# Re-timing three pieces of work at the seam between projections and attention

## The chip, the cores and the metric

The kernel runs on one core of a Trainium2 chip. The metric is the time of one execution on the device, in microseconds (us); less is better. The core has five engines that run side by side, each working through its own list of instructions in order: TensorE (PE, matrix products), VectorE (DVE), ScalarE (ACT), GpSimd (POOL) and SyncE (SP), which here issues every transfer. An engine that meets an instruction whose inputs are not ready stands still, and everything behind that instruction waits with it. The same is true of the list of transfers on SP.

## The reference

The input `x` has 1024 rows of 512 columns. It is normalized by rows, and the result goes into an attention and into a feed-forward network whose weights are stored as small integers with scales. The output is `x` plus the attention, multiplied by a gate made of the network:

```python
def reference(x, Wq, Wk, Wv, Wo, q_norm_w, k_norm_w, gate_w, ..., down_s):
    xn = layernorm(x)
    # attention: 32 query heads, 8 key/value heads of 128 columns
    q, k, v = heads(xn @ Wq.T), heads(xn @ Wk.T), heads(xn @ Wv.T)
    q, k = rmsnorm(q, q_norm_w), rmsnorm(k, k_norm_w)
    scores = q @ k.T / sqrt(128)            # four query heads share one key head
    bias = where(col > row, -1e30, slope[head] * (col - row))
    s = (softmax(scores + bias) @ v) @ Wo.T
    # feed-forward
    gate, up, down = (dequantize(w, scale, zero) for ...)
    g = silu((silu(xn @ gate) * (xn @ up)) @ down)
    return x + s * g
```

## The kernel before

**Precision.** Each product is made of three float16 products: an operand is split into a high half and a low half (the rest), and high x high, high x low and low x high are added up. `mm3` issues these three, at lines 114, 115 and 116, so all large products after the feed-forward part carry these line numbers; the tile names (`ps_q`, `s`, `av`, `op`) tell them apart.

**Stages.** The feed-forward part runs first, to about 215 us. Then come twelve projections, in groups of three: keys and values of two heads (`kv`), and queries of the one and of the other key group (`q`). They are numbered 0 to 11: kv0, q0, q1, kv1, q2, q3, and so on; number 9 is kv3, number 10 is q6, and number 11, the last, is q7. Each has eight row tiles, so there are 96 tiles (`TILES`). Attention follows in 256 steps, one for each pair of a unit (key group, block of 256 queries, head) and a tile of 128 queries. A key group has 32 steps. The first eight steps of the softmax run ahead: they are interleaved with the 16 tiles of the last two projections (`early_tile`, one step per two tiles), so the loop over `step` starts at step 8.

**What a projection leaves to be finished.** After the four tiles of one half, `queue_half` puts the finishing of that half on a calendar (`finishing`, a list per value of `clock[0]`, which advances by one with every tile or step). The finishing consists of `inverse` (VectorE, over the sums of squares `ss` that ScalarE made), for projections 0 to 9 `root` (ScalarE's square root), `newton` (POOL), then for each tile `normalize` (POOL, L650), `halves` (VectorE, L662 and L663, for keys L661 too), one clock later `transposed` (a transposing DMA on SP, L671) and two clocks after that `store` (a DMA to DRAM, L676 for queries, L678 for keys). The tile `f`, which ScalarE's copy at L592 fills and `halves` reads last, comes from four rotating buffers.

For the last projection the calendar is set by hand: `LAST_ROOTS` and `LAST_PAIRS` give the entry at which a half's root or a tile's halves are made, counted from `TILES`. Step 8 runs at clock `TILES`, so an entry n falls into step n + 8. The pairs of the last projection stay in SBUF, and `last_queries` transposes them directly when `LAST_QUERIES` says.

**A step of attention.** `scores` (TensorE, tile `s`), `biased` (VectorE, L896), `exponentials` (ScalarE, L902), `split_hi` (ScalarE, L921, the high half of p), `split_lo` (VectorE, L930, the low half), the latter ending with the transposition of p on SP (L938, or L933 for the first query block, tile `pT`). Nine steps after its scores, `values` multiplies transposed p with the values (tile `av`); `heads_hi` and `heads_lo` split the outcome (L964, L969), and `out_proj` multiplies it with the output weights, which are loaded by `load_wo` (L852), scaled on POOL (L855) and split on ScalarE (L861) and POOL (L862). In each key group from the second to the last but one the order of query blocks is 2, 3, 0, 1, with eight steps each.

**The main loop.** It prepares projection k + 1 (`prepare`: norms at tile 1, the split of its weights from tile 2 to 6), loads the weights of projection k + 2 in four quarters at tiles 0 to 3 (L500) and squares them on ScalarE from tile 5 on (L508). At the start of projection 9 it loads keys (L817), values (L821) and the first queries (L825) of attention. The weights of projections and half of the tiles `pT` share the two buffers of the tag "wide".

Of the kernel before, what the change touches and what calls it, by code (L numbers as in the profile page):

```python
# [10 lines left out]
F32 = mybir.dt.float32  # L11
# [10 lines left out]
P = 128  # L22
# [9 lines left out]
HT = NT // 2  # L32
# [21 lines left out]


LAST_ROOTS = {1: 24, 0: 36}
LAST_PAIRS = {4: 46, 5: 78, 6: 110, 7: 142, 2: 174, 3: 221, 0: 224, 1: 229}
LAST_QUERIES = {4: 217, 5: 219, 6: 225, 7: 227, 2: 233, 3: 235, 0: 241, 1: 243}

WO_SPLIT = 6  # L60
# [16 lines left out]
def attention_gated_by_ffn_kernel(ctx, tc, x, gu_w, gu_z, gu_s, dn_w, dn_z, dn_s, wq, wkv, wo, qnw, knw, out):  # L77
# [397 lines left out]
    clock, finishing = [0], {}  # L475
# [7 lines left out]
    def defer(steps, f):  # L483
        finishing.setdefault(clock[0] + steps, []).append(f)
# [4 lines left out]
    class Projection:  # L489
# [92 lines left out]
        def tile(self, t):  # L582
            n, half, r = self.n, t // HT, t % HT
            if r == 0:
                self.f[half] = fq.tile([P, HT, n, HD], F32, tag="f", name=f"f_{self.name}_{half}", bufs=4)
                self.ss[half] = fq.tile([P, HT, n], F32, tag="ss", name=f"ss_{self.name}_{half}", bufs=3)
                self.jk = wp.tile([P, NH, HD], BF16, tag="jk", name=f"jk_{self.name}_{half}")
            ps = ps1("o" if t % 2 else "m", f"ps_{self.name}_{t}")
            rows = slice(t * P, (t + 1) * P)
            for j in range(KT):  # L590
                mm3(ps, (xth[:, j, rows], xtl[:, j, rows]), (self.wh[:, j, :], self.wl[:, j, :]), j == 0, j == KT - 1)
            se.copy(self.f[half][:, r], ps[:, : n * HD].rearrange("p (g d) -> p g d", g=n))  # L592
            for i in range(n):
                se.activation(
                    self.jk[:, i],
                    ps[:, i * HD : (i + 1) * HD],
                    AF.Square,
                    scale=STEEPER[i] / Q_SCALE if self.kind == "q" else 1.0,
                    accum_out=self.ss[half][:, r, i : i + 1],
                )  # L600
            if self.kind == "kv":
                if t == 0:
                    self.v16 = vp16.tile([P, 2, NT, 2, HD], F16, tag="v16", name=f"v16_{self.i}")
                v16 = self.v16[:, :, t]
                vp = ps[:, 256:512].rearrange("p (g d) -> p g d", g=2)
                se.copy(v16[:, :, 0, :], vp)
                defer(1, lambda: ve.tensor_tensor(v16[:, :, 1, :], vp, v16[:, :, 0, :], ALU.subtract))
                if t == NT - 1:
                    defer(3, self.store_values)
# [5 lines left out]
        def inverse(self, half):  # L615

            m = HT * self.n
            a = fq.tile([P, m], F32, tag="ms", name=f"ms_{self.name}_{half}")
            y = fq.tile([P, m], F32, tag="inv", name=f"inv_{self.name}_{half}")
            w = fq.tile([P, m], F32, tag="nwt", name=f"nwt_{self.name}_{half}")  # L620
            ve.scalar_tensor_tensor(
                a.rearrange("p (t g) -> p t g", t=HT),
                self.ss[half],
                1.0 / HD,
                self.eps.unsqueeze(1).to_broadcast([P, HT, self.n]),
                ALU.mult,
                ALU.add,
            )
            self.inv[half] = (y, a, w)
            if not self.by_root:  # L630
                rsqrt_seed(a, y)
# [48 lines left out]
    projections = []  # L680
# [102 lines left out]
    def queue_half(p, half):  # L783

        last = p is projections[-1]

        def due(steps, i, f):
            if last and i is None:
                c = TILES + LAST_ROOTS[half]
            elif last:  # L790
                c = TILES + LAST_PAIRS[half * HT + i] - 4
            else:
                c = clock[0] + (i or 0)
            finishing.setdefault(c + steps, []).append(f)

        due(0, None, lambda: p.inverse(half))
        if p.by_root:
            due(1, None, lambda: p.root(half))
            due(2, None, lambda: p.newton(half, True))
        else:  # L800
            for i in range(3):
                due((i + 1) // 2, None, lambda i=i: p.newton(half, i == 0))
        later = int(p.by_root)
        for i in range(HT):
            t = half * HT + i
            due(4 + later, i, lambda t=t: p.halves(t))
            due(2 + later, i, lambda t=t: p.normalize(t))
# [7 lines left out]
    def load_keys(g):  # L815
        kT[g] = ap1.tile([P, NT, 2, P], F16, tag="kT", name=f"kT{g}")
        sp.dma_start(kT[g].rearrange("p t a k -> p t (a k)"), kd[g // 2][:, g % 2])  # L817

    def load_values(g):
        vT[g] = ap1.tile([P, NT, 2, HD], F16, tag="vT", name=f"vT{g}")  # L820
        sp.dma_start(vT[g].rearrange("p t a d -> p t (a d)"), vd[g])  # L821

    def load_queries(g, qb):
        qT[g, qb] = ap1.tile([P, NQT, 2, NH, P], F16, tag="qT", name=f"qT{g}_{qb}", bufs=2)
        sp.dma_start(  # L825
            qT[g, qb].rearrange("p t a g q -> p t (a g q)"), qd[g][qb * NQT : (qb + 1) * NQT].rearrange("t p c -> p t c")
        )
# [77 lines left out]
    def split_hi(u, qt):  # L905
# [14 lines left out]
            p16[u] = both  # L920
        se.activation(p16[u, qt][:, :, 0, :], pf[u, qt], AF.Copy, scale=scale[:, qt : qt + 1])  # L921

    def split_lo(u, qt):
        p, h16 = pf.pop((u, qt)), p16.pop((u, qt))
        nk = p.shape[1]
        if qt == 0:
            pool, tag = (wide, "wide") if u % 4 < 2 else (pt_pool, "pT")
            pT[u] = pool.tile([P, NT, 2, QB], F16, tag=tag, name=f"pT{u}", bufs=2)
        hi, lo, scale = h16[:, :, 0, :], h16[:, :, 1, :], rows16[u][3][:, qt : qt + 1]
        ve.scalar_tensor_tensor(lo, p, scale, hi, ALU.mult, ALU.subtract)  # L930
        if u in p16:
            if qt == NQT - 1:
                sp.dma_start_transpose(  # L933
                    pT[u][:, :NQT].rearrange("p t a (i q) -> p (t a i) q", i=NQT),
                    p16.pop(u).rearrange("p t a i k -> p (t a i k)"),
                )
            return
        sp.dma_start_transpose(  # L938
            pT[u][:, :nk, :, qt * P : qt * P + P].rearrange("p t a q -> p (t a) q"), h16.rearrange("p t a k -> p (t a k)")
        )  # L940

# [175 lines left out]
    last_ps = None  # L1117
    relative(0)
    for k, p in enumerate(projections):
        if k == len(projections) - 3:  # L1120
            load_keys(0)
            load_values(0)
            for qb in blocks[0][1]:
                load_queries(0, qb)
        for t in range(NT):
            prepare(k + 1, t)
            if k + 2 < len(projections):
# [4 lines left out]
                    projections[k + 2].squares(i)  # L1132
            if t == HT:
                p.undo()
            if (k, t) == (len(projections) - 3, HT + 1):
                wo_squares_sums()

# [59 lines left out]
```

## Time and profile before

| | |
|---|---|
| three runs | 1060.75, 1058.24, 1058.08 us; median 1058.24 |
| profiled execution | 1055.74 us, its span 1054.0 us |
| engines busy, share of the span | PE 95%, DVE 84%, ACT 76%, POOL 40% |
| matmuls of the projections q0 to q7 | 238 to 482 us |
| scores of step 0, 8, 32, 64 start at | 432.5, 481.1, 540.1, 608.2 us |
| SP busy issuing, of each 10 us from 470, 480, 490 us | 10.0, 9.1, 9.5 us |

In the rows of the profile, "waits" name the engine and line that waited, behind the arrow the one that released it, then the total in us, how often, and the longest. Rows of the timeline have the start, the duration, the engine and line, the operation with its output and inputs, and in square brackets the idle time of the engine just before, with what ended it. SPq is SP's queue of transfers: its durations are the time that issuing one took, not the time of the transfer. "Windows" give, for a stretch of time, its length and the busy time of PE, PEld (weight loads), DVE, ACT and POOL with the count of instructions, then the granted clock of TensorE, the busy share of the DMA engines and their GB/s.

### The profile page before, as it was taken

To read this page: it belongs to the slowest core of one execution; us is meant where nothing else is said; L and a number is where in the kernel's file an instruction comes from. 1 tells how busy PE (TensorE), PEld (TensorE's weight loads), DVE (VectorE), ACT (ScalarE), POOL (GpSimd) and SP (SyncE) were. 2 spreads that over 40 slices of the span, in tenths; PEclk is the share of its full clock that TensorE was granted. 3 is DMA by queue.
4 is the path that set the end of the run, shared out by engine and by line. 5 is a ranking of instruction groups with operands and counts; after the bars stand their busy time and mean duration, and the time that the engine had idled before them with its cause. 6 is when DMAs were issued, how large, how long until landed. Compare 5 with 4: busy or idle time off the path is not lost.

```text
span 1054.0 us, 18375 instructions
## 1 busy us (share of the span) xinstructions
PE 999.9 (95%) x5913; PEld 585.8 (56%) x5913; DVE 882.7 (84%) x1745; ACT 800.5 (76%) x2160; POOL 420.8 (40%) x407
## 2 busy tenths in 40 slices
PE   7899899999999999898899999999999999999996
PEld 5444367854444444344566567566666666665563
DVE  7888997626888877887789899898998998979986
ACT  5777645778878787787789688797997888968862
POOL 1688654115555647371324215113142151340732
PEclk8999999999999999999999999999999999999999
DMA  6032349536998989989999999899998998999995
GB/s 204 30 120 91 99 135 307 203 121 170 216 274 176 250 205 242 263 181 225 222 193 222 190 200 219 168 227 203 191 215 185 215 210 185 219 227 200 232 188 131
DMA packets 455039, 204.39 MB, mean 194 GB/s; under 512 B 401506, under 2 KB 411038, under 8 KB 454942
## 3 DMA queue, kind: packets, MB, share of 16 engines
q1 hardware_dynamic: 454942, 203.21, 86.8%
q8 instruction: 46, 0.75, 0.3%
q14 instruction: 51, 0.42, 0.1%
HBM read 77.32 MB, written 27.27 MB: 99 GB/s over the span
## 4 chain that ended last, share of the span: by engine, by line
PE 59%; DVE 13%; ACT 10%; DMA 9%; issue 6%; POOL 2%; SPq 0%; DVEq 0%; ACTq 0%; POOLq 0%
PE gu_ps L267 6%; DMA pT<-p 5%; PE s L114 4%; PE s L116 4%; PE s L115 4%; PE op L116 3%; PE op L115 3%; PE op L114 3%; PE ps_q L115 3%; PE ps_q L116 3%; PE ps_q L114 3%; PE av L114 3%; PE av L115 3%; PE av L116 3%; DVE pf L896 2%
## 5 line engine op out<-in xcount | busy, mean ns | idle before, releaser
L930 DVE SCALAR_TENSOR_TENSOR p<-pf,row,p 128x1024 f16<-128x1024 f32 (+7 forms) x256 | 224.9, 878 | 21.4 <-ACT p L921 18.4
L902 ACT ACTIVATE pf<-pf,row 128x1024 f32<-128x1024 f32 (+7 forms) x256 | 197.4, 771 | 41.4 <-DVE row L896 36.9
L896 DVE CUSTOM_DVE_ANT_0 pf<-s,trel,cs 128x1024 f32<-128x1024 f32 (+7 forms) x256 | 207.0, 809 | 20.8 <-PE s L116 20.4
L921 ACT ACTIVATE p<-pf,row 128x1024 f16<-128x1024 f32 (+7 forms) x256 | 196.6, 768 | 6.9 <-DMA pT<-p 2.1
L114 PE MATMUL av<-pT,vT 128*128 128x256 f16 (+1 forms) x640 | 168.4, 263 | 21.0 <-DMA pT<-p 21.0
L115 PE MATMUL av<-pT,vT 128*128 128x256 f16 (+1 forms) x640 | 168.4, 263 | 0.0
L116 PE MATMUL av<-pT,vT 128*128 128x256 f16 (+1 forms) x640 | 168.2, 263 | 0.0
L114 PE MATMUL s<-kT,qT 128*128 128x512 f16 (+3 forms) x384 | 125.6, 327 | 4.8 <-DVE row L896 4.8
L115 PE MATMUL s<-kT,qT 128*128 128x512 f16 (+3 forms) x384 | 125.6, 327 | 0.0
L116 PE MATMUL s<-kT,qT 128*128 128x512 f16 (+3 forms) x384 | 123.9, 327 | 0.0
L855 POOL TENSOR_SCALAR wor<-wor,rvs 128x512 f32<-128x512 f32 x32 | 51.9, 1623 | 169.4 <-DMA wor<-in_wo 148.9
L115 PE MATMUL ps_q<-wl_q,xth 128*128 128x512 f16 x256 | 97.0, 379 | 3.6 <-DVE wl_q L565 3.6
L114 PEld LDWEIGHTS <-vT 128*128 128x128 f16 x640 | 62.9, 98 | 62.6 <-issue 13.0
L116 PE MATMUL ps_q<-wh_q,xtl 128*128 128x512 f16 x256 | 97.0, 379 | 0.0
L114 PE MATMUL ps_q<-wh_q,xth 128*128 128x512 f16 x256 | 97.0, 379 | 0.0
L114 PE MATMUL op<-woh,oh 128*128 128x512 f16 x248 | 94.0, 379 | 0.0
L115 PE MATMUL op<-wol,oh 128*128 128x512 f16 x248 | 94.0, 379 | 0.0
L116 PE MATMUL op<-woh,ol 128*128 128x512 f16 x248 | 94.0, 379 | 0.0
L964 ACT ACTIVATE oh<-av 128x256 f16<-128x256 f32 x128 | 47.7, 373 | 54.8 <-PE av L116 53.9
L115 PEld LDWEIGHTS <-vT 128*128 128x128 f16 x640 | 62.9, 98 | 40.9 <-issue 2.4
L650 POOL TENSOR_TENSOR f_q<-f_q,inv_q 128x512 f32<-128x512 f32 x64 | 80.1, 1275 | 1.0
L862 POOL TENSOR_TENSOR wol<-wor,woh 128x512 f16<-128x512 f32 x32 | 50.3, 1572 | 60.9 <-ACT woh L861 59.1
(194 smaller groups left out, 2263.9 us busy)
## 6 DMA issues: line engine op xcount, KB each, us to landing
qd<-tr_q SPq DMA_DIRECT2D x56, 256.0 KB, 3.4
qT<-qd SPq DMA_DIRECT2D x28, 512.0 KB, 4.5
wq<-in_wq SPq DMA_DIRECT2D x32, 256.0 KB, 4.0
wo_sq<-in_wo SPq DMA_DIRECT2D x8, 1024.0 KB, 8.9
wor<-in_wo SPq DMA_DIRECT2D x32, 256.0 KB, 3.5
gui<-in_gu_w SPq DMA_DIRECT2D x13, 512.0 KB, 4.0
wkv<-in_wkv SPq DMA_DIRECT2D x16, 256.0 KB, 4.0
vd<-v SPq DMA_DIRECT2D x8, 512.0 KB, 4.6
```

The costliest lines, as they stand in the source:

```text
L114: te.matmul(ps, lhsT=lh, rhs=rh, start=first, stop=False)
L115: te.matmul(ps, lhsT=lh, rhs=rl, start=False, stop=False)
L116: te.matmul(ps, lhsT=ll, rhs=rh, start=False, stop=last)
L267: te.matmul(banks[j][:, k, :], lhsT=w[:, j, ws], rhs=x[:, j, k * 512 : k * 512 + 512], start=x is xth, stop=x is xtl)
L650: ge.tensor_tensor(f, f, ib, ALU.mult)
L855: ge.tensor_scalar(wor[g, i], wor[g, i], rvs[:, g : g + 1], None, ALU.mult)
L862: ge.tensor_tensor(wol[g, i], raw, woh[g, i], ALU.subtract)
L896: ve.tensor_tensor_reduce(p, ps, trel[g][:, S - w :], cs[:, hh : hh + 1], 3e38, ALU.add, ALU.min, least[:, c])
L902: se.activation(p, p, AF.Exp, bias=least[:, c], scale=-1.0, accum_out=total[:, c])
L921: se.activation(p16[u, qt][:, :, 0, :], pf[u, qt], AF.Copy, scale=scale[:, qt : qt + 1])
L930: ve.scalar_tensor_tensor(lo, p, scale, hi, ALU.mult, ALU.subtract)
L964: se.activation(oh, av_ps[u], AF.Copy, scale=1.0 / P_SCALE)
```

## The change

Four edits go together. The finishing of q6's second half (the last projection but one) gets a calendar of its own: roots at entry 32, pairs at entries 44, 60, 76 and 92; the pairs of q7's second half and its third tile move from 46, 78, 110, 142, 174 to 108, 124, 140, 156, 172. The finishing of projections 0 to 9 is spread: the inverse one clock later, the root at 2 instead of 1, the Newton step at 4 instead of 2, normalization and halves two clocks later; `ss`, `ms`, `inv` and `nwt` get four buffers. As long as the clock is below `TILES`, the transposition of p is deferred by one clock, which puts it into the tile after the next. Keys and first queries are loaded at tile 4 of projection 9 instead of ahead of its first tile, and values at tile 4 of projection 10.

```diff
-LAST_PAIRS = {4: 46, 5: 78, 6: 110, 7: 142, 2: 174, 3: 221, 0: 224, 1: 229}
+LAST_PAIRS = {4: 108, 5: 124, 6: 140, 7: 156, 2: 172, 3: 221, 0: 224, 1: 229}
+
+LATE_ROOTS = 32
+LATE_PAIRS = [44, 60, 76, 92]
...
-                self.ss[half] = fq.tile([P, HT, n], F32, tag="ss", name=f"ss_{self.name}_{half}", bufs=3)
+                self.ss[half] = fq.tile([P, HT, n], F32, tag="ss", name=f"ss_{self.name}_{half}", bufs=4)
...
-            a = fq.tile([P, m], F32, tag="ms", name=f"ms_{self.name}_{half}")
-            y = fq.tile([P, m], F32, tag="inv", name=f"inv_{self.name}_{half}")
-            w = fq.tile([P, m], F32, tag="nwt", name=f"nwt_{self.name}_{half}")
+            a = fq.tile([P, m], F32, tag="ms", name=f"ms_{self.name}_{half}", bufs=4)
+            y = fq.tile([P, m], F32, tag="inv", name=f"inv_{self.name}_{half}", bufs=4)
+            w = fq.tile([P, m], F32, tag="nwt", name=f"nwt_{self.name}_{half}", bufs=4)
...
         last = p is projections[-1]
+        late = p is projections[-2] and half == 1
 
         def due(steps, i, f):
-            if last and i is None:
+            if late:
+                c = TILES + (LATE_ROOTS if i is None else LATE_PAIRS[i] - 4)
+            elif last and i is None:
                 c = TILES + LAST_ROOTS[half]
...
-        due(0, None, lambda: p.inverse(half))
+        due(int(p.by_root), None, lambda: p.inverse(half))
         if p.by_root:
-            due(1, None, lambda: p.root(half))
-            due(2, None, lambda: p.newton(half, True))
+            due(2, None, lambda: p.root(half))
+            due(4, None, lambda: p.newton(half, True))
...
-        later = int(p.by_root)
+        later = 3 * p.by_root
...
+    def transpose_pairs(dst, pairs):
+        if clock[0] < TILES:
+            defer(1, lambda: sp.dma_start_transpose(dst, pairs))
+        else:
+            sp.dma_start_transpose(dst, pairs)
+
     def split_lo(u, qt):
...
-        sp.dma_start_transpose(
+        transpose_pairs(
             pT[u][:, :nk, :, qt * P : qt * P + P].rearrange("p t a q -> p (t a) q"), h16.rearrange("p t a k -> p (t a k)")
         )
...
-        if k == len(projections) - 3:
-            load_keys(0)
-            load_values(0)
-            for qb in blocks[0][1]:
-                load_queries(0, qb)
         for t in range(NT):
...
             if t == HT:
                 p.undo()
+                if k == len(projections) - 3:
+                    load_keys(0)
+                    for qb in blocks[0][1]:
+                        load_queries(0, qb)
+                elif k == len(projections) - 2:
+                    load_values(0)
```

More of the change, by code (lines that the diff above doesn't have):

```diff
@@ L937, in split_lo @@
             return
-        sp.dma_start_transpose(
+        transpose_pairs(
             pT[u][:, :nk, :, qt * P : qt * P + P].rearrange("p t a q -> p (t a) q"), h16.rearrange("p t a k -> p (t a k)")
```

## The prediction

> **What bounds the kernel now.** I read the page's busy shares first, then the waits of TensorE alone, then every TensorE gap after the feed-forward part in order of time, and last each engine and the SP queue around the two largest clusters.
>
> ```profile
> PE 999.9 (95%) x5913; PEld 585.8 (56%) x5913; DVE 882.7 (84%) x1745; ACT 800.5 (76%) x2160; POOL 420.8 (40%) x407
> PE av L114 <- DMA pT<-p: 21.0, 15, 3.3
> PE s L114 <- DVE row L896: 4.8, 6, 2.0
> PE ps_q L115 <- DVE wl_q L565: 3.6, 1, 3.6
> ```
>
> TensorE has work nearly always, so only its gaps can be won back. After 220 us there are two clusters that this change touches: one of 3.64 us at 430, where q6 (the last projection but one) begins, and eight between 482 and 531, at the entrance of attention: 3.31, 2.43, 1.80, 0.64 and 0.27 us (8.45) before `av` for transposed p, and 0.78, 0.66, 0.28 (1.72) before `s`. Later there is one gap of 0.16 to 2.18 us per key group.
>
> ```profile
> 409.26 0.75 SPq L817 DMA_DIRECT2D kT<-kd  x1
> 410.06 0.44 SPq L821 DMA_DIRECT2D vT<-vd  x1
> 410.54 0.43 SPq L825 DMA_DIRECT2D qT<-qd  x1
> ...
> 422.38 0.59 SPq L500 DMA_DIRECT2D wq<-in_wq  x1
> ...
> 426.61 0.63 ACT L508 ACTIVATE sq_q<-wq 128x512 bf16<-128x512 f32 x1 [6.27 <-DMA wq<-in_wq]
> 429.27 0.20 DVE L640 RECIPROCAL inv_kv<-inv_kv 128x8 f32<-128x8 f32 x1 [2.63 <-ACT inv_kv L635]
> 430.15 0.38 PE L115 MATMUL ps_q<-wl_q,xth 128*128 128x512 f16 x1 [3.64 <-DVE wl_q L565]
> ```
>
> Read upwards, this is the first cluster: ScalarE stands 6.27 us before the squares of q7's weights, whose last quarter was issued at 422.38 behind keys, values and queries; so its square root for kv3 is late, VectorE stands 2.63 us before the reciprocal, and the last low half of q6's weights, queued behind that, is late for TensorE.
>
> ```profile
> 485.71 1.27 DVE L930 SCALAR_TENSOR_TENSOR p<-pf,row,p 128x1024 f16<-128x1024 f32 x1
> 488.34 1.29 SPq L671 DMA_TRANSPOSE tr_q<-q  x1
> 489.73 0.52 SPq L676 DMA_DIRECT2D qd<-tr_q  x1
> 490.35 1.30 SPq L671 DMA_TRANSPOSE tr_q<-q  x1
> 491.74 0.78 SPq L852 DMA_DIRECT2D wor<-in_wo  x1
> 492.62 2.98 SPq L938 DMA_TRANSPOSE pT<-p  x1
> 497.11 0.40 PE L114 MATMUL av<-pT,vT 128*128 128x256 f16 x1 [3.31 <-DMA pT<-p]
> 498.00:500.00 2.00, 2.00 (x10) 1.29 (x9) 1.59 (x4) 1.97 (x5) 0.86 (x1) 0.50 1.01 305
> ```
>
> The second cluster: p's low half is ready at 486.98, but its transposition enters the queue only at 492.62, behind q6's own; `av` waits 3.31 us for it. The last line (a window: PE, PEld, DVE, ACT, POOL busy, then granted clock, DMA share, GB/s) shows the clock at 0.50 right behind that gap.
>
> **The change, part by part.**
>
> *Weights ahead of keys.* Three loads (0.75 + 0.44 + 0.43 = 1.6 us of SP) leave the front of q7's weight loads. Two query transpositions among those loads held SP 3.08 and 2.68 us against a median of 1.31 for L671; if the 1.5 MB in flight are why, that is 3.1 us more. The last quarter is then issued 4.7 us earlier and ScalarE's 6.27 shrink to 1.6; the 3.64 us gap closes. Bounds: the keys and queries now sit behind tile 4 of kv3. If SP is as late there as at its last weight load (422.38 for a place at 405.4, where kv3's first matmul runs, + 3 tiles of 2.59 = 413.2, so 9.2), they go at 425.0 and, with the 7.7 us to landing that these queries took, are there at 432.7; the first scores (432.52 now) would want them at 428.9. That loses 3.8: gain between -0.2 and 3.64. I take 3.6, since the front loads are the direct cause, and SP is relieved by just them.
>
> *Finishing two tiles later for kv and q projections 0 to 9* (inverse, root and Newton step get a tile more each). It removes VectorE's waits of 1.54 for the squares, 0.71 and 2.63 for the roots; these belong to the same late chain and are not counted again. Two finishes of q5 move out of kv3's tiles into q6's: 2 x (0.46 + 0.79) us of VectorE, 2 x (1.31 + 0.52) of SP. In q6's tiles SP stands still about 7 of 50 us and VectorE has gaps of 0.75 to 1.51 us: no cost while that cover holds, 3.7 us without it. What is late next are the `f` buffers: of four, each is wanted again by ScalarE's copy (L592) four halves on. The closest pair in the trace is 387.75 (fourth finish) to 397.81 (copy), 10.06 us; two tiles are 5.2, so 4.9 remain: cost 0. The larger pools of `ss`, `ms`, `inv`, `nwt` only avoid waits.
>
> *The first transpositions of p a tile back.* SP now stops in program order before L938 until VectorE has made the low half (3.6 us once). With the others in front this idleness goes; what TensorE sees of it is in the next part, so 0 here. The price: the transpositions of the first five tiles of p come up to two tiles (6.4 us) later. The fourth, now issued at 477.01, is wanted by `av` of step 11 at 490, so the delay is covered; uncovered it would be a gap of at most 6.4.
>
> *Half of q6 out of the entrance.* Four pairs leave it. SP loses four L671 (1.28 + 1.38 + 1.29 + 1.30 = 5.25) and four L676 (0.53 + 0.52 + 0.57 + 0.58 = 2.20), together 7.45 us; VectorE 4 x 1.25, POOL 4 x 1.28. The last of the first four pairs of p was issued at 500.83 for a low half ready at 491.33, 9.5 us late, so SP's lateness is larger than the relief and the relief is worth its full length. What can be won in all is 8.45 + 1.72, and the half clock: from 497.11 until it was back at some 500.1 (0.97 in 500 to 502) 3.0 us of matmuls ran at 0.50, which cost 1.5, so 11.7. Bounds: 11.7 above; below, ScalarE may take the place: from 481.1 to 500 it was busy 15.32 us where TensorE without gaps and half clock would need 18.9 - (0.78 + 0.66 + 0.28 + 3.31 + 1.5) = 12.4; 2.9 of the 7.45 would stay, 4.5 are left. I take 7.4, since ScalarE's own waits there (6.5 us before `woh`, whose load stands in the same queue) go too.
>
> [...]
>
> [...]
>
> *Nine finishes inside attention instead of five.* A finish at entry n runs at step n + 8, since the clock stands at TILES in step 8. Before, five ran at phase 22 of a group's 32 steps (54, 86, ...); now five at phase 20 (52, 84, 116, 148, 180), and four more at phase 4 (68, 100, 132, 164). The windows are the four blocks of the fourth group:
>
> ```profile
> 678.28:695.54 17.26, 17.26 (x124) 10.86 (x122) 16.97 (x35) 15.84 (x35) 2.57 (x1) 1.00 1.03 194
> ...
> 716.69:734.33 17.64, 17.48 (x147) 13.14 (x145) 14.36 (x40) 11.91 (x35) 7.24 (x8) 1.00 1.08 206
> ```
>
> Phase 20 lies in the third block, where VectorE has 3.3 us free: 0. Phase 4 lies in the first, where VectorE is busy 16.97 of 17.26: 1.25 us more, of which its waits before the group's gap (0.21 + 0.28 + 0.30 in the third group) absorb 0.79; 0.46 each arrives at that gap, 1.8 in all. Bounds: 0 (SP's slack hides it), and 4 x 1.25 plus SP's 1.83 for the two pairs of q6 among them, 8.7. POOL's normalizations (1.28 us) lie two steps ahead, on an engine 40% busy; behind each SP transposition stands p's next one, which in that block is held 1.30 us in a 2.16 us step.
>
> **Sum.** -3.6 - 7.4 + 1.8 = -9.2. The profiled execution took 1055.74 (span 1054.0 and 1.74 around it), which gives 1046.5; the median of the runs is 2.5 above that execution, so 1049.0 against 1058.24.
>
> **Rivals.** *Only the seam is mended* (0.18): the entrance stays as long, because ScalarE, at 15.32 of 18.9 us, or VectorE before `s` now ends last. For it: ScalarE's share; against: its waits there hang on the same queue. Only the half clock goes, as the gaps come in smaller pieces: -3.6 - 1.5 + 1.8 gives 1054.9. *The keys come too late* (0.10): it doesn't do at the seam what it says, and the wait moves from q6's weights to the first scores; +0.2 - 7.4 + 1.8: 1052.8. For it: SP was 9.2 us late there; against: mostly through the loads that are moved away. *Slower* (0.08): finishing two tiles later makes ScalarE's copies wait for `f` buffers, in each of the 20 halves, and PSUM and TensorE behind them. The spare 4.9 us must vanish; it decides from 9.2 / 20 = 0.46 us per half; at 1 us the time is 1049.0 + 20 = 1069. For it: two of the spare tiles are spent. Against it: ten to fifteen us in every half now, with VectorE busy at most 84% and POOL 57% of each 50 us from 250 to 400.
>
> **How the numbers follow.** The forecast has 0.60, with its own range 1043 to 1052 (its bounds: 3.64 + 11.7 without cost, 1042.9, and 3.6 + 4.5 with 1.8 of cost, 1051.9; the cost of 8.7 with the full gains gives 1055.9). The remaining 0.04 goes to causes not seen. The range 1043 to 1056 takes in the first two rivals. 0.3% is 3.2 us, about what a measurement can tell from no change: faster is below 1055.1, so forecast, late keys and half of the first rival, 0.79 (0.60 + 0.10 + 0.09); within, 0.09 and 0.02 of the unseen, 0.11; slower, 0.08 and the other 0.02, 0.10.
>
> **What would show it.** Right: no gap at the first matmuls of q6 and ScalarE's wait before L508 below 2 us; no L671 between tile 4 of q7 and step 12; `av` waits under 2.5 us in the whole entrance; no half-clock window there; one group's gap longer by some 0.5 us in the third to sixth group. Wrong: `s` waiting for `kT` or `qT` at its first matmul, new gaps at every fourth tile of the projections, or the entrance's gaps reappearing before `s` with VectorE named.

## The result, and the profile after

The changed kernel takes **1064.09 us** (median of 20 runs, 1058.67 to 1067.94) against 1057.5 for the kernel before in the same comparison (20 runs): a ratio of **1.0055**, 95% interval 1.0037 to 1.0073. It is slower, by about 6 us, where 9 us less were forecast. The profiled execution took 1064.09, its span 1062.3; before it was 1055.74 and 1054.0, the latter 1.8 us faster than its kernel's median.

Two starts in the table of the profile before are one step late: 540.1 and 608.2 belong to steps 33 and 65; steps 32 and 64 start at 538.1 and 606.55. The windows of the fourth group in the prediction are displaced by one step in the same way. Below, every start is that of the step named. "Projections" is the time from the first product of a projection to the first scores, "entrance" that from the scores of step 8 to those of step 32, "later" that from there to the start of the last scores. "Half clock" is the sum of the stretches in the trace's clock record, between the first projection and the last scores, in which TensorE was granted half speed.

| profiled execution, us | before | after | |
|---|---|---|---|
| projections | 215.15 | 212.57 | -2.6 |
| step 0 to 8 | 48.62 | 48.61 | |
| entrance | 56.96 | 57.85 | +0.9 |
| third key group (steps 64 to 96) | 70.10 | 74.55 | +4.5 |
| fourth key group | 68.08 | 71.43 | +3.4 |
| later, in all | 489.44 | 500.46 | +11.0 |
| half clock | 6.8 | 20.5 | +13.7 |

The four stretches of the table (projections, step 0 to 8, entrance, later) are 9.3 us longer together. At half speed 13.7 us lose 6.8 of them, and TensorE's busy time grows by as much, 6.6; the rest, 2.7, is gaps. First the page's busy shares and the waits of TensorE after (line, what it waited for, total, times, longest):

```profile
PE 1005.1 (95%) x5913; PEld 587.7 (55%) x5913; DVE 885.2 (83%) x1745; ACT 801.4 (75%) x2160; POOL 409.9 (39%) x407
PE av L117 <- DMA pT<-p: 25.0, 15, 3.6
PE s L117 <- DVE row L902: 6.0, 7, 2.0
```

The wait of q6 for its weights is gone, but `av` waits 4 us more for transposed p. The seam, from the timelines of SP, ScalarE and TensorE after:

```profile
418.06 0.67 SPq L503 DMA_DIRECT2D wq<-in_wq  x1
...
420.87 0.80 SPq L823 DMA_DIRECT2D kT<-kd  x1
422.44 0.63 ACT L511 ACTIVATE sq_q<-wq 128x512 bf16<-128x512 f32 x1 [1.67 <-DMA wq<-in_wq]
429.61 0.38 PE L117 MATMUL s<-kT,qT 128*128 128x512 f16 x1
```

The last quarter of the weights is issued 4.3 us earlier, ahead of the keys, and ScalarE waits 1.67 us for it instead of 6.27. The first scores come at 429.61 instead of 432.52. The entrance after, from the timelines of VectorE, SP and TensorE, and two windows:

```profile
468.53 0.43 DVE L665 CAST q<-f_q 128x512 f16<-128x512 f32 x1 [3.83 <-DMA tr_kv<-k]
472.93 1.28 DVE L942 SCALAR_TENSOR_TENSOR p<-pf,row,p 128x1024 f16<-128x1024 f32 x1
478.41 1.64 SPq L931 DMA_TRANSPOSE pT<-p  x1
480.14 1.81 SPq L674 DMA_TRANSPOSE tr_q<-q  x1
482.64 2.63 SPq L679 DMA_DIRECT2D qd<-tr_q  x2
485.32 4.18 SPq L931 DMA_TRANSPOSE pT<-p  x2
490.09 0.37 PE L117 MATMUL av<-pT,vT 128*128 128x256 f16 x1 [3.39 <-DMA pT<-p]
486.00:490.00 4.00, 0.70 (x5) 0.29 (x3) 3.81 (x7) 2.79 (x7) 0.00 (x0) 0.77 1.11 218
490.00:494.00 4.00, 3.91 (x17) 2.38 (x18) 1.08 (x3) 2.68 (x4) 0.52 (x1) 0.50 1.15 238
```

VectorE stands 3.83 us before a cast for a free buffer of halves (`a16`), which the transposition of a key tile must first read out. The low half of the fourth tile of p is ready at 474.2, but its transposition goes out at 485.32, 8.3 us later than in the kernel before (477.01), and `av` of step 11 waits for it. The clock is then half for 6.8 us. Inside attention the largest gap is in the third group; SP's queue there and the low half of step 78's p, first before, then after:

```profile
632.39 4.12 SPq L938 DMA_TRANSPOSE pT<-p  x2
...
649.75 1.57 DVE L930 SCALAR_TENSOR_TENSOR p<-pf,row,p 128x896 f16<-128x896 f32 x1 [0.32 <-ACT p L921]
652.12 6.20 SPq L938 DMA_TRANSPOSE pT<-p  x2
662.01 0.27 PE L114 MATMUL av<-pT,vT 128*128 128x256 f16 x1 [2.18 <-DMA pT<-p]
606.55:676.65 70.10, 67.92 (x483) 43.87 (x481) 62.62 (x140) 57.90 (x134) 18.59 (x14) 1.00 1.01 199
```

```profile
619.92 2.26 SPq L674 DMA_TRANSPOSE tr_q<-q  x1
...
625.47 0.83 SPq L679 DMA_DIRECT2D qd<-tr_q  x1
633.88 4.55 SPq L933 DMA_TRANSPOSE pT<-p  x2
649.42 1.57 DVE L942 SCALAR_TENSOR_TENSOR p<-pf,row,p 128x896 f16<-128x896 f32 x1 [0.32 <-ACT p L927]
653.83 7.74 SPq L933 DMA_TRANSPOSE pT<-p  x3
663.20 0.39 PE L117 MATMUL av<-pT,vT 128*128 128x256 f16 x1 [3.55 <-DMA pT<-p]
606.17:680.72 74.55, 70.96 (x483) 45.09 (x480) 63.34 (x142) 58.05 (x134) 19.59 (x15) 0.95 0.99 202
```

The pair of q6 at step 68 puts 2.26 + 0.83 us into a full queue. From the group's start, the transposition of step 78's p that was issued after 45.57 us now goes after 47.66. VectorE is not what is late: the low half of that tile is ready 44.8 us after the group's start in both kernels, and SP issues its transposition 0.8 us later before and 2.8 us later after. The gap grows from 2.18 to 3.55, and 6.8 us at half clock follow it. By the two windows the same products keep TensorE busy 3.0 us longer (67.92 and 70.96), which is the clock, and it stands idle 1.4 us longer: 4.5 together, the group's growth.

### The profile page after: what moved, and what is told of

Its sections match the earlier page's. It is cut to its first block, busy times and chain, and to the rows that moved or that the text cites. A ratio compares the mean times of both kernels' runs of the same rounds, so it can differ in the third digit from the quotient of the medians.

```text
span 1062.3 us, 18370 instructions
## 1 busy us (share of the span) xinstructions
PE 1005.1 (95%) x5913; PEld 587.7 (55%) x5913; DVE 885.2 (83%) x1745; ACT 801.4 (75%) x2160; POOL 409.9 (39%) x407
## 4 chain that ended last, share of the span: by engine, by line
PE 62%; DVE 13%; DMA 8%; ACT 8%; issue 7%; POOL 1%; DVEq 0%; SPq 0%; ACTq 0%; POOLq 0%
PE gu_ps L270 6%; DMA pT<-p 6%; PE s L117 4%; PE s L119 4%; PE s L118 4%; PE ps_q L118 4%; PE ps_q L117 4%; PE ps_q L119 4%; PE av L117 3%; PE op L117 3%; PE op L118 3%; PE av L118 3%; PE av L119 3%; PE op L119 3%; DVE pf L902 3%
## 5 line engine op out<-in xcount | busy, mean ns | idle before, releaser
L117 PE MATMUL av<-pT,vT 128*128 128x256 f16 (+1 forms) x640 | 169.9, 265 | 25.1 <-DMA pT<-p 25.0
L976 ACT ACTIVATE oh<-av 128x256 f16<-128x256 f32 x128 | 47.7, 373 | 59.1 <-PE av L119 58.8
L653 POOL TENSOR_TENSOR f_q<-f_q,inv_q 128x512 f32<-128x512 f32 x64 | 75.1, 1195 | 0.9
L981 DVE SCALAR_TENSOR_TENSOR ol<-av,oh 128x256 f16<-128x256 f32 x128 | 53.4, 417 | 24.4 <-ACT oh L976 24.2
```

The lines of the kernel that those rows point to most:

```text
L117: te.matmul(ps, lhsT=lh, rhs=rh, start=first, stop=False)
L653: ge.tensor_tensor(f, f, ib, ALU.mult)
L976: se.activation(oh, av_ps[u], AF.Copy, scale=1.0 / P_SCALE)
L981: ve.scalar_tensor_tensor(ol, av_ps.pop(u), 1.0 / P_SCALE, oh, ALU.mult, ALU.subtract)
```

## The experiments

Each ratio is against the kernel before on the same chip; "after" itself stands at 1.0055 [1.0037, 1.0073]. Two ratios whose intervals overlap are not told apart by them. Stage times are from one profiled execution each, which lies up to 4.6 us off its kernel's median, so a difference of one or two us in one stage says little. "3rd + 4th" is the sum of the third and fourth key group. Edits are named as parts: *loads*, *delay* (projections 0 to 9 finished two tiles later), *deferral* (of p's first transpositions), *late* (nine late pairs). Names with u_ undo one part of the changed kernel, names with o_ have only the parts named.

| kernel | parts it has | ratio [95%] | projections | entrance | 3rd + 4th | half clock |
|---|---|---|---|---|---|---|
| before | none | 1 | 215.2 | 57.0 | 138.2 | 6.8 |
| after | all | 1.0055 [1.0037, 1.0073] | 212.6 | 57.9 | 146.0 | 20.5 |
| u_shift | without delay | 0.9980 [0.9957, 1.0003] | 212.9 | 51.2 | 140.0 | 6.8 |
| u_defer | without deferral | 1.0021 [0.9993, 1.0048] | 212.6 | 56.5 | 143.3 | 13.7 |
| u_late | without late | 1.0050 [1.0030, 1.0070] | 213.3 | 62.9 | 137.9 | 17.1 |
| u_loads | without loads | 1.0039 [1.0015, 1.0062] | 216.6 | 51.3 | 145.0 | 13.7 |
| o_shift | delay alone | 1.0060 [1.0036, 1.0085] | 217.9 | 60.5 | 137.9 | 17.1 |
| o_late | late alone | 1.0014 [0.9985, 1.0042] | 217.0 | 50.7 | 146.6 | 17.1 |
| o_loads | loads alone | 1.0006 [0.9987, 1.0025] | 213.6 | 60.0 | 137.5 | 13.7 |
| o_late_loads | late and loads | 1.0008 [0.9986, 1.0031] | 211.4 | 51.6 | 145.0 | 17.1 |
| kv3_early | all, delay not for kv3 | 1.0094 [1.0067, 1.0121] | 213.0 | 58.2 | 146.2 | 17.1 |
| shift_all | all, q6's first half delayed too | 1.0052 [1.0026, 1.0077] | 213.2 | 58.5 | 145.9 | 13.7 |
| shift_06 | all, delay for 0 to 6 | 1.0064 [1.0041, 1.0087] | 216.6 | 51.9 | 145.7 | 13.7 |
| act_stores | all, stores on ScalarE | 1.0044 [1.0025, 1.0063] | 215.1 | 53.6 | 141.4 | 10.2 |
| pool_stores | all, stores on POOL | 1.0035 [1.0014, 1.0056] | 212.0 | 53.2 | 143.5 | 13.7 |
| slots | late at other places, loads, deferral | 0.9939 [0.9912, 0.9967] | 212.0 | 53.2 | 136.7 | 0 |
| slots_oldloads | same without loads | 0.9953 [0.9929, 0.9977] | 215.0 | 50.7 | 136.7 | 6.8 |
| slots_nodefer | same without deferral | 0.9940 [0.9919, 0.9960] | 211.4 | 51.3 | 136.6 | 3.4 |
| o_slots | late at other places, alone | 0.9964 [0.9940, 0.9988] | 215.6 | 50.3 | 136.9 | 10.2 |
| slots_act | slots, stores on ScalarE | 0.9994 [0.9974, 1.0014] | 211.4 | 51.9 | 137.4 | 10.2 |

**Each part undone.** Deferral undone:

```diff
-        if clock[0] < TILES:
-            defer(1, lambda: sp.dma_start_transpose(dst, pairs))
-        else:
-            sp.dma_start_transpose(dst, pairs)
+        sp.dma_start_transpose(dst, pairs)
```

> The changed kernel, but p is transposed at once as before. Theory D (the deferral is at fault): in the changed kernel the fourth transposition of p was issued at 485.3 us though its low half was ready at 474.1, and `av` stood 3.39 us, with 6.8 us of half clock behind it; without the deferral it goes out before 480, so that gap and its half clock leave: 3.4 + 3.4 less, 5 to 7 us faster than the changed kernel. Rival S (the two-tile shift is at fault: keys of kv3 and queries of q6 come due together and share five buffers): the same low halves stay late, at most 1.5 us faster.

It is 0.34% below the changed kernel, with overlapping intervals. The 3.39 us gap before `av` is gone; ahead of its place 0.28 us stand before `s`, and the first gap before `av` is now 2.12 us. The entrance is only 1.4 us shorter. Delay undone:

```diff
-        due(int(p.by_root), None, lambda: p.inverse(half))
+        due(0, None, lambda: p.inverse(half))
...
-            due(2, None, lambda: p.root(half))
-            due(4, None, lambda: p.newton(half, True))
+            due(1, None, lambda: p.root(half))
+            due(2, None, lambda: p.newton(half, True))
...
-        later = 3 * p.by_root
+        later = int(p.by_root)
```

> The changed kernel, but projections 0 to 9 are finished as early as before. Theory S: VectorE's waits of 1.67 and 3.83 us for transpositions of keys in q7's tiles go, p's third low half comes some 4 us earlier, 3 to 6 us faster than the changed kernel. Theory D: SP still gets the fourth transposition two tiles late, less than 1.5 us faster; and the 3.64 us gap at q6 stays closed under both if the weights ahead of the keys closed it, or comes back in part if the shift did.

This is the large one: 0.75% below the changed kernel, entrance 6.7 us shorter, no half clock from the first projection to 950 us. The entrance of after and of u_shift (windows), and the sixth tile of p in each (VectorE's low half, SP's transposition):

```profile
478.22:536.07 57.85, 48.95 (x349) 33.32 (x348) 42.21 (x103) 44.38 (x116) 13.29 (x11) 0.91 1.07 218
483.31 1.27 DVE L942 SCALAR_TENSOR_TENSOR p<-pf,row,p 128x1024 f16<-128x1024 f32 x1
490.74 2.95 SPq L933 DMA_TRANSPOSE pT<-p  x1
```

```profile
478.21:529.37 51.16, 45.17 (x350) 31.35 (x349) 40.82 (x100) 42.86 (x111) 13.75 (x11) 1.00 1.04 217
482.32 1.26 DVE L942 SCALAR_TENSOR_TENSOR p<-pf,row,p 128x1024 f16<-128x1024 f32 x1
484.40 2.88 SPq L933 DMA_TRANSPOSE pT<-p  x1
```

Of the 6.7 us, 3.8 are longer busy time of TensorE, which is the half clock, and 2.9 are gaps. The low half comes 1.0 us later with the delay; SP takes it up 6.2 us after it is ready instead of 0.8. Late pairs undone, with the old table:

```diff
-LAST_PAIRS = {4: 108, 5: 124, 6: 140, 7: 156, 2: 172, 3: 221, 0: 224, 1: 229}
+LAST_PAIRS = {4: 46, 5: 78, 6: 110, 7: 142, 2: 174, 3: 221, 0: 224, 1: 229}
...
-        late = p is projections[-2] and half == 1
+        late = False
```

> The changed kernel, but q6's second half is finished in q7's tiles as before, and q7's pairs at their old entries. Theory L (the pairs inside attention are at fault, by SP and the half clock): the gap of the third group falls from 3.55 to some 2.2 and its 6.8 us of half clock go, the fourth group's gaps fall from 3.2 to below 1.5: 6 us faster inside attention. Against that the entrance gets four transpositions and four stores back, 7.4 us of SP: by the prediction's step that costs 7 us there, so about the changed kernel's time in all; if the relief was worth nothing, 6 us faster in all.

The entrance is 5.0 us longer and the later part 9.0 shorter (491.45); by the ratio the two cancel within the intervals. Old load order:

```diff
+        if k == len(projections) - 3:
+            load_keys(0)
+            load_values(0)
+            for qb in blocks[0][1]:
+                load_queries(0, qb)
         for t in range(NT):
...
-                if k == len(projections) - 3:
-                    load_keys(0)
...
```

> The changed kernel, but keys, values and queries are loaded ahead of q7's weights again. If this edit closed the 3.64 us gap at the start of q6 (the prediction's step): that gap is back and ScalarE waits over 4 us for the weights, 3 to 4 us slower than the changed kernel, unless the entrance swallows it. Rival (the two-tile shift closed it by itself): no gap there, within 1 us.

The projections are 4.1 us longer again and the entrance 6.5 shorter: what the loads win at the seam is lost at the entrance. This kernel has the delay, and yet its entrance is 51.3. Its step 32 starts 316.6 us after the first product of a projection, against 316.3 in o_late below, which has neither delay nor deferral, so with the old load order and the late pairs the delay shows no price up to there.

**Do two streams meet?** The delayed half of kv3 and q6's first half now finish in the same tiles of q7 and share five `a16` buffers. In kv3_early the delay holds for projections 0 to 8:

```diff
+            self.spread = k < 3 * HKV // 2 - 3
...
-        later = 3 * p.by_root
+        later = p.by_root + 2 * self.spread
```

> The changed kernel with the two-tile shift kept for projections 0 to 8 and taken back for kv3 (number 9) alone. Theory C (collision: the shift puts kv3's last keys into the same tiles of q7 as q6's first queries, two transpositions and two stores per tile on SP and five shared buffers): kv3 alone made it, so this is as fast as without any shift, 1052 to 1055. Rival G (the shift costs wherever it is, q5's last finishes in q6's tiles included): 1058 to 1064.

It was no faster than the changed kernel (1.0094 from six runs, the intervals touch), with the entrance at 58.2. But q5's delayed half now met kv3's; so in shift_all q6's first half was delayed as well, by three tiles, and those two streams no longer meet:

```diff
-        later = 3 * p.by_root
+        later = 3 * p.by_root + 3 * (p is projections[-2] and half == 0)
```

> The changed kernel with the first half of q6 finished three tiles later as well, so that its four tiles no longer fall into the same tiles of q7 as the delayed last half of kv3. If the price of the delay is the meeting of these two streams: VectorE's waits of 1.67 and 3.83 us for a free half buffer at the casts of k and q go, the third row tile of p is transposed well before 485, the entrance (scores of step 8 to step 32) falls from 57.9 us to 52 to 54, and the time is 0.3 to 0.6% below the changed kernel's (about 1.000 of before). Rival, the delay costs something wherever it is put, because it only moves transpositions and stores towards those of p: the entrance stays at 57 us or more, the av gap moves to a later step, and the ratio to before stays at 1.004 to 1.007.

VectorE's waits of 1.67 and 3.83 shrank to one of 0.68, and the entrance was 58.5 all the same, with a gap of 4.59 us before `av`. This is no clean test: q6's four delayed pairs now go out until 56.2 us after the first scores instead of 50.5, ahead of the fifth transposition of p. o_shift, next, says more: it pays the price of the delay although VectorE waits for no buffer of halves there from the first scores to step 32. So these waits are not needed for the price.

**Parts alone.** The delay alone and the late pairs alone, in the kernel before (edits as above, the other way round; the larger pools stay in all):

> The kernel before with the two-tile delay of projections 0 to 9 alone (with its fourth buffers). If the two meeting streams are the price: the same waits at the casts of k and q appear, the entrance is 4 to 7 us longer than the 57.0 us of before, the rest of attention is as before, ratio 1.003 to 1.007. If the delay costs only where the transposition of p is deferred too: ratio 1.000, entrance 57. If it mends the seam by itself (VectorE no longer waits for the late square root of kv3): the 3.64 us gap at the first products of q6 is below 1 us as well, and the ratio is 3 us lower than by the entrance alone.

1.0060: the delay alone costs 6 us (0.0060 x 1057.88 = 6.3, interval 3.8 to 9.0). The 3.64 us gap shrinks to 1.58, another of 1.44 appears at 388, and p's transpositions are late:

```profile
482.80 1.95 SPq L930 DMA_TRANSPOSE pT<-p  x1
502.62 0.39 PE L117 MATMUL av<-pT,vT 128*128 128x256 f16 x1 [5.61 <-DMA pT<-p]
```

This transposition, the fourth, comes 48.7 us after the first scores; before it was 44.5 (477.01 - 432.52). SP issues 19 transpositions of q and k between 431 us and it, before 16. In this profile the projections are 2.7 us longer and the entrance 3.5.

> The kernel before with only the second half of q6 and the pairs of q7 moved into attention; loads, finishing of the others and transpositions of p as before. The prediction put this at -7.4 + 1.8 = -5.6 us (ratio 0.9947). If the relief at the entrance is about 5 us and the nine finishes inside attention cost 6 to 9 us, as the runs so far suggest: entrance (step 8 to 32) 50 to 52 us against 57.0, step 32 to the last scores 495 to 500 us against 489.4, ratio 1.000 to 1.004, with a half clock behind a gap in the third group. The 3.64 us gap at q6 stays in either case.

The entrance was 6.3 us shorter and the third and fourth group 8.4 longer.

Late pairs with loads, and loads alone:

> The changed kernel without the two-tile shift and without the deferral: left are the late half of q6 and the weights ahead of the keys. Theory D (the deferral delays p's transpositions into the entrance, by 4.8 us where the shift was on): faster than without the shift alone, 1048 to 1051. Rival: without the collision SP is early enough in either order, within 1.5 us of 1053.3; or the deferral keeps SP from standing before low halves, then slower, 1055.

> The kernel before with one edit: q7's weights are loaded ahead of keys and queries, values later. The prediction's step: the 3.64 us gap at q6 goes, 3 to 4 us faster than before. Rival E (time won at the seam is lost at the entrance, because SP and ScalarE, not TensorE, set when p is transposed; taking this edit back from the changed kernel made it 3.6 us faster): the gap goes, step 32 starts no earlier, within 1 us of before or slower.

o_late_loads, beside u_shift, is the deferral without the delay: 1.0008 and 0.9980, so there it looked like a gain of 0.28%, with overlapping intervals. o_loads is no change: the 3.64 us gap is gone and the first scores come 1.8 us earlier, but SP's transpositions do not. Its fourth and fifth transposition of p and the gap behind them, of the SP and the TensorE timeline:

```profile
477.56 2.88 SPq L930 DMA_TRANSPOSE pT<-p  x1
485.71 1.71 SPq L930 DMA_TRANSPOSE pT<-p  x1
497.36 0.39 PE L117 MATMUL av<-pT,vT 128*128 128x256 f16 x1 [5.14 <-DMA pT<-p]
```

In the kernel before they went out at 477.01 and 484.73. TensorE arrives earlier and waits for the same transpositions: 5.14 us where it was 3.31.

**Is it SP's queue?** From 420 to 490 us SP is busy issuing for 6.6 to 9.3 of each 10 us after, and for 7.9 to 9.5 before, in its program's order. A delay that ends before this stretch, and two kernels with the stores of the last four projections on another engine's queue:

```diff
-                sp.dma_start(qd[self.i][t], tr.rearrange("p c t -> p (c t)"))
+                (se if self.k >= 8 else sp).dma_start(qd[self.i][t], tr.rearrange("p c t -> p (c t)"))
```

(`kd` in the same way; in pool_stores `ge` in place of `se`; shift_06 has `self.spread = k < 7` in kv3_early's edit.)

> The changed kernel with the two-tile delay for projections 0 to 6 alone; q4, q5 and kv3 are finished as before. New theory: what the delay costs is SP's queue. From the loads of keys at 421 to the fourth transposition of p SP is busy 8 to 10 of each 10 us, and the delay puts two more finished tiles (20 transpositions of q and k instead of 18) into this stretch, so that the fourth transposition of p goes out 55.7 us after the first scores instead of 49.1. Then a delay that ends before that stretch costs nothing: fourth transposition of p at 48 to 50 us, entrance (step 8 to 32) 51 to 53 us against 57.9, ratio to before 0.996 to 1.000. Rival, the delay costs in every projection: entrance 57 or more, ratio 1.004 to 1.007.

> The changed kernel with the stores of finished q and k of the last four projections issued by ScalarE's queue instead of SP. SP loses some 20 issues of 0.55 us, 11 us, between 421 and 483. If SP's queue is the price of the delay: the fourth transposition of p goes out at most 51 us after the first scores (now 55.7), entrance 51 to 54 us against 57.9, ratio 0.997 to 1.002. Rival, VectorE or ScalarE sets the entrance and SP only follows: the transpositions go out earlier, but the entrance stays at 56 or more, now with gaps before the scores; ScalarE may also stand behind a store whose transposition is late, and then it is longer than 58.

> As the kernel with the stores on ScalarE's queue, but on POOL's. SP is relieved by the same 11 us. If SP's queue is the price: entrance 51 to 54 us, ratio 0.997 to 1.002, unless POOL (normalization of the last projections behind the stores) becomes late. Rival as there: 56 or more.

All three entrances came as expected if SP's queue is the price: 51.9, 53.6 and 53.2 us. The fourth transposition of p went out 49.6 us after the first scores in shift_06 and 49.4 in act_stores; in pool_stores it still took 53.3. All three ratios missed. In shift_06 the projections are 4.0 us longer: in the tiles behind the last delayed projection the weights of q5, kv3 and q6 come late.

```profile
386.72 0.38 PE L118 MATMUL ps_q<-wl_q,xth 128*128 128x512 f16 x1 [1.10 <-DVE wl_q L569]
409.30 0.38 PE L118 MATMUL ps_kv<-wl_kv,xth 128*128 128x512 f16 x1 [1.24 <-DVE wl_kv L584]
431.67 0.38 PE L118 MATMUL ps_q<-wl_q,xth 128*128 128x512 f16 x1 [0.98 <-DVE wl_q L569]
```

With the stores moved, steps 0 to 8 took 50.2 (ScalarE) and 53.9 us (POOL) instead of 48.6, and new gaps stand before `s` behind VectorE: 4.11 us at 490.63 in the former, 2.18 at 471.56 in the latter. SP's queue was relieved: the sixth transposition of p goes out 0.1 us after its low half in both, against 6.2 after. But that low half itself comes 58.8 and 61.5 us after the first scores instead of 55.0, and step 32 starts 318.9 and 319.2 us after the first product of a projection, against 319.0 in the changed kernel. So the delay makes SP late at the entrance, but that SP's queue alone makes the 6 us is not shown: relieving it won nothing in all.

**Place or number of the late pairs?** In slots all nine lie in the third blocks of their groups, none at phase 4; the delay is undone:

```diff
-LAST_PAIRS = {4: 108, 5: 124, 6: 140, 7: 156, 2: 172, 3: 221, 0: 224, 1: 229}
+LAST_PAIRS = {4: 142, 5: 172, 6: 174, 7: 204, 2: 206, 3: 221, 0: 224, 1: 229}
...
-LATE_PAIRS = [44, 60, 76, 92]
+LATE_PAIRS = [44, 76, 108, 140]
```

> The changed kernel without the two-tile shift, and with q6's four late pairs only in the light third block of a key group (entries 44, 76, 108, 140) and q7's behind them (142, 172, 174, 204, 206), none in the first block. Theory L (a late pair in the first block pushes SP's queue and lengthens the gap before the fourth block): the third and fourth group's gaps shrink to what the kernel before has (69 us per group), 2 to 4 us faster than without the shift alone (1053.3). Rival: SP's slack hides these pairs, as the prediction had it, within 1.5 us of 1053.3.

> The kernel before with only q6's second half and q7's pairs moved into the third blocks of the key groups (entries 44, 76, 108, 140 and 142, 172, 174, 204, 206); loads, finishing of the others and transpositions of p as before. If the relief of the entrance is 5 to 6 us and the pairs cost nothing in the third blocks: entrance (step 8 to 32) 50 to 52 us against 57.0, the rest of attention 489 to 492 us against 489.4, the 3.64 us gap at q6 stays, ratio 0.993 to 0.996. Rival: half-clock windows come whatever the slots, the rest of attention is 495 or more, ratio 0.998 to 1.002.

Both are faster than the kernel before and than the changed one. The third group of slots and of o_late (windows), and slots' gap in it:

```profile
601.52:670.27 68.75, 68.07 (x482) 43.89 (x480) 62.62 (x140) 58.00 (x134) 17.86 (x14) 1.00 1.05 211
655.63 0.27 PE L117 MATMUL av<-pT,vT 128*128 128x256 f16 x1 [0.68 <-DMA pT<-p]
```

```profile
602.44:677.54 75.10, 70.71 (x483) 44.74 (x481) 63.34 (x142) 58.05 (x134) 18.83 (x15) 0.95 1.01 200
```

o_slots and o_late differ in the places alone: with the same nine pairs the third and fourth group take 136.9 or 146.6 us. They take 140.0 to 146.6 in the eleven kernels with pairs at phase 4, and 136.6 to 138.2 in the nine without.

The three kernels that vary slots:

> The fastest so far (no delay, q6's and q7's late pairs only in the light third blocks at entries 44, 76, 108, 140, 142, 172, 174, 204, 206, transposition of p deferred) with the loads of keys, values and queries where they were before. If the gain at the seam is given back at the entrance, as it was in the kernel before with the load order alone: the gap of 2.5 to 3.6 us at q6 is back, the entrance is 2 to 4 us shorter, ratio 0.992 to 0.996. If the load order counts here, where the entrance has been relieved: 2.5 to 3.5 us slower than that kernel, ratio 0.9965 to 0.9975.

> The fastest so far (no delay, late pairs in the third blocks, new load order) with the first transpositions of p not deferred. If the deferral is worth something without the delay (0.28% between two earlier kernels of another load of pairs): 0.9955 to 0.998, with the entrance 1 to 3 us longer than 53.2. If that difference came from half-clock windows alone: the same ratio, 0.992 to 0.996, and the same entrance within 2 us.

> The fastest so far (no delay, late pairs only in the light third blocks, new load order, deferral) with the same stores on ScalarE's queue. If SP's queue is still what the entrance waits for (its av gaps there are 4 to 5 us in all): entrance 50 us against 53.2 and ratio 0.989 to 0.992 against 0.994. If ScalarE's time counts more: the same or slower, 0.994 to 0.998.

The deferral is worth nothing here (0.9940 against 0.9939). The loads can't be told apart from nothing: 0.9953 against 0.9939 with overlapping intervals, and 2.5 of the 2.9 us by which slots starts its scores earlier are lost at the entrance. Stores on ScalarE made it worse: steps 0 to 8 grew to 52.8 us. The best medians are slots_nodefer, 1047.89 against 1054.43, and slots, 1048.29 against 1054.6.

## Why the prediction was wrong

**The sign: the two-tile delay, put at 0.** The step that failed is "no cost while that cover holds, 3.7 us without it", and of the two cases the first was taken. The cover was read too large: 420 to 470 us do have 7 idle us, but they reach into q7's tiles; in q6's own 29.4 us SP stood idle 4.2. And it did not hold: with kv3's part taken back (kv3_early) the entrance stays at 58.2, with q4's and q5's too (shift_06) it is 51.9. Measured: 6.3 us alone [3.8, 9.0], above the 3.7, and 0.75% between the changed kernel and the one without it. In the changed kernel it shows as SP's lateness for p's transpositions (6.2 us instead of 0.8 for the sixth), and 3.8 of the 6.7 us at the entrance are half clock, which the term did not have. The prediction also did not follow the two finishes of kv3 that the same delay moves from q6's tiles into q7's; by kv3_early they are not the price by themselves. The `f` buffers, the rival "slower through f buffers", were not it: ScalarE's idle time before its copies of q is 22.8 us in all after, 25.1 before. The slower side had 0.10, on the wrong mechanism. How the 6 us divide between SP's queue, later low halves and late weights of the projections stays open.

**The deferral, put at 0 because covered.** "Wanted by `av` of step 11 at 490, so the delay is covered" failed in this kernel: the transposition went out at 485.32 and the gap was 3.39 us, within the 6.4 named for it. In these runs it costs only beside the delay (0.34%, u_defer); without the delay the two pairs of kernels differ by 0.28% and 0.01% in its favour, which is not told apart from nothing.

**The seam, -3.6.** The mechanism at the seam was right (the gap is gone, ScalarE's wait is 1.67, below the 2 named), and the first scores came 2.6 to 2.9 us earlier in the changed kernel, 1.8 with this part alone. What was wrong is that the gain reaches the end: SP's transpositions did not move forward with the scores. Alone the part gives 1.0006 [0.9987, 1.0025].

**Half of q6 out of the entrance, -7.4.** Right in mechanism and nearly in size at the entrance: 6.3 us in o_late, 6.7 in o_slots, 5.0 beside the delay.

**Nine finishes inside attention, +1.8.** The place was right (phase 4), the size and the wait not. The term counted VectorE's time, 0.46 us a pair, and let SP's queue into the upper bound only; the rows show SP late behind a foreign transposition and VectorE in time. It cost 7.8 us in the third and fourth group after and 8.4 alone, near the upper bound of 8.7, and more than it over the whole later part (11.0 and 10.8). The bound left the clock out, and that was the larger part in the third group: 3.0 of 4.5 us.

In sum: -3.6 became about 0, the delay 0 became +6, and relief and late pairs together -5.6 became +1.5 [-1.6, +4.4] (o_late), which has 10.2 us more at half clock than the kernel before. These parts alone add up to some 8 us where 5.8 were measured for all together, a difference that lies within their intervals.

## What to carry to other kernels

A delay on a calendar moves work at every seam, the last one too: follow it to where the stream ends, and look at the queue there, in its own order. Time won ahead of an in-order queue that is full can be lost again behind it, as the new load order shows (alone: first scores 1.8 us earlier, ratio 1.0006). When work is moved into a loop, its place within the period can decide: with the same nine finishes the third and fourth group were 8 us longer than before when some stood in the first blocks, and no longer when all stood in the third.

## What the hardware showed that was not expected

The prediction took half clock as a matter of single gaps. The windows of half clock start on a raster of 3.413 us: in after, 508.66, 662.26 and 1000.18 lie 6, 51 and 150 such lengths behind 488.18, and before, 991.65 lies 145 behind 496.72. What they went with in the 20 profiles is how busy TensorE was in the raster window ahead. Taking every such window between 230 us and the last products that itself ran at full clock: with TensorE busy below 40% of it, 57 of 57 were followed by half clock; from 40 to 50%, 14 of 32; above 50%, none of some 4600. Two raster windows of after and the one behind each, then the two that the 3.64 us gap at q6 fell into before:

```profile
505.26:508.67 3.41, 1.41 (x11) 0.84 (x9) 2.04 (x5) 1.24 (x3) 2.01 (x1) 1.00 1.14 203
508.67:512.08 3.41, 3.41 (x15) 2.00 (x14) 1.68 (x4) 3.04 (x9) 2.68 (x3) 0.50 1.07 234
658.85:662.27 3.42, 0.80 (x8) 0.39 (x6) 1.63 (x6) 2.24 (x8) 1.31 (x2) 1.00 1.38 169
662.27:665.68 3.41, 2.48 (x11) 1.64 (x12) 0.00 (x0) 0.00 (x0) 0.00 (x0) 0.50 1.04 192
```

```profile
424.99:428.41 3.42, 1.52 (x8) 0.59 (x6) 1.34 (x3) 1.77 (x6) 0.00 (x0) 1.00 1.20 226
428.41:431.82 3.41, 1.67 (x8) 0.78 (x8) 2.51 (x7) 3.38 (x18) 1.94 (x5) 1.00 1.12 281
```

The window of after that holds a gap of 2.00 us (1.41 of 3.41 busy) was followed by half clock, and so was the one of before, 493.33 to 496.74, that holds most of the 3.31 us gap (0.47 busy). The gap of 3.64 us was split over two windows (1.52 and 1.67 busy), and the clock stayed at 1.00. Over the 20 profiles the time from the first projection to the last scores rises by 1.0 us with each us of half clock (correlation 0.87): 0.4 of it is longer busy time of TensorE, the clock itself, and 0.6 is idle time, the gaps that come with it. With slots, which has no half clock in this stretch, this time is 804.1 us, with after 819.5.
